# Layer 0 of a decoder: norms, transposes and rotary of the experts stage's first two groups in the cross attention's last turns

## The chip, the cores and the metric

The kernel runs on one core of one Trainium2 chip. Its time is the device time of one execution, in microseconds (us); the figure used is the median of several runs. The core's engines are called by their short names in the profile: PE (TensorE, matrix products and transposes), PEld (its weight loads), DVE (VectorE), ACT (ScalarE), POOL (GpSimd) and SP (SyncE, which here only issues transfers).

## The reference

A decoder of two layers works on x, an array of 32 sequences of 100 tokens with 256 features, all in float32. Each layer adds three sub-layers, each on a normed copy of x: a causal self attention, a cross attention, and a mixture of experts.

```python
x = x + attn(layernorm(x), ...)            # layer 0: causal, 16 heads of 16
x = x + xattn(ctx, layernorm(x), mask, ...)# 4 heads of 64, 361 context rows of 192
x = x + ffn(layernorm(x), ...)             # attention with rotary, then 8 experts
x = x + attn1(...); x = x + xattn1(...); x = x + ffn1(...)   # layer 1
```

Layer 0's cross attention norms the context and the latents (x) with gains, makes keys and values from both (361 + 100 rows), normalises each head of queries and keys by its root mean square, takes a masked softmax, and projects back. Layer 0's third sub-layer is a block of its own: rotary on the features, a causal attention of 16 heads whose queries and keys come from the rotated input and whose values come from the unrotated one, then a layer norm, a gate over 8 experts of which the two best count, and a last layer norm:

```python
q_in = apply_rope(x);  q, k, v = q_in @ Wq.T + bq, q_in @ Wk.T + bk, x @ Wv.T + bv
x1 = ln(x + softmax(causal(q @ k.T / 4)) @ v @ Wo.T + bo)
out = ln(x1 + sum_over_top2(gate * (x1 @ expert_w[e].T + expert_b[e])))
```

## The kernel before, in words

x stays in SBUF as eight tiles `xs[g]`, one for each group g of four sequences (100 token rows, four sequences, 256 features). The six sub-layers follow each other as stages: `a0` (self attention), `x0` (cross attention), `f0` (experts), then `a1`, `x1` and the experts of layer 1. The change touches `x0` and `f0` and a helper that `a0` and `f0` share.

**How order is set.** Inside a block `with in_order():` the instructions of PE, DVE, ACT and POOL go onto their engines in the order in which the program writes them, by hand. Across engines, and where a buffer is used again, the tile framework adds the waits. Outside of such blocks, and for SP, its scheduler places instructions. PSUM is cut into two `sc` tiles of two banks and four `mm` tiles of one bank, taken in turn. SBUF is given out by pools: a tile of a tag takes the next of that tag's buffers and waits until the last reader of what lay there is done. A pool opened where another was closed waits in the same way. Weight pools `w0`, `w1`, `w2` and so on are opened on alternating sides of SBUF; their loads are put on SP's queue when the pool is opened (`weight` and `plain`, transfers at L256 and L261).

**Stage x0.** `w2`, the pool with the experts stage's weights, is opened just ahead of `x0` and filled then, the 2 MB matrix of the experts (`f0_we`), the experts' biases (`f0_eb`) and the rotary table (`rope`) among them. The loop of `x0` has turns n from -4 to 32 (L851). In turn n, work of several sequences is interleaved, as a pipeline over b: keys of n+1 are transposed (`keys_turned`, PE L717 and L725, copies to kT by ACT L720 and to qT by DVE L728), the second half of n's softmax is divided (`divided`, DVE reciprocal L783 and POOL product L784), sequence n-1 is projected and added to x (`output`, PE L223, DVE L828, POOL L829), keys of n+2 are squared (ACT L681), and their roots taken (DVE L687, POOL L691), keys and values of n+3 made from latents (`own_keys_values`, ACT L671), n's weights transposed (`turn_weights`, PE L793, ACT L796), contexts of n+4 to n+6 normed and transposed, scores of n+1 made (`scores`, PE L751), n's weighted sums taken (`sums`, PE L807), and n+1's softmax begun (DVE L770, ACT L774). The turn ends with

```python
at(n + 1, exponentials, 1)
if out_:
    out_()
at(n + 1, divided, 0)
```

So `divided(n+1, 0)` is the last thing of turn n and `divided(n+1, 1)` an early one of the next turn, and their reciprocals are neighbours on DVE. From turn 26 on the pipeline has no new contexts to load, from turn 29 on no new keys to make.

**Stage f0.** `heads_attention` (L275) is the attention with 16 heads. Its prologue makes group 0's input by `norm(0, part)` for four parts, q and k of group 0 in four steps m (0 and 1 are q, 2 and 3 are k; PE L223, evacuations ACT L305 and L315), values and scores of sequence 0 and its softmax (DVE L365 and L376, POOL L377, ACT L382), and then all four parts of `norm(1, part)`. Its loop over turns s works on the weights of sequence s and the scores of s+1, and spreads q and k of the next group over turns: q in turns 0 and 1 of a group, both k in turn 2.

`norm(g, part)` in `f0` has these parts: part 0, statistics (four times DVE L161 and L162, DVE L170 and L173, POOL L174 and L176); part 1, the scaling of x to xl (four ACT L192); part 2, eight transposes (PE L945) with two copies to xlT (ACT L948); part 3, the rotary, four DVE instructions (L956, twice L958, L961), whose result xrT is what q and k are made from. The experts' matrix is first used in turn 9 of the stage, by `experts` (PE L1073).

Of the kernel before, what the change touches and what calls it, by code (L numbers as in the profile page):

```python
# [10 lines left out]
F32 = mybir.dt.float32  # L11
# [7 lines left out]
P = 128  # L19
# [47 lines left out]
def kernel(ctx: ExitStack, tc: tile.TileContext, io: dict, out: bass.AP):  # L67
# [207 lines left out]
    def heads_attention(pool, w, wo, bias, norm, turn, res, fill):  # L275
# [171 lines left out]
        with in_order():  # L447
            for part in range(4):
                norm(0, part)
# [9 lines left out]
            for part in range(4):  # L459
                norm(1, part)  # L460
            for s in range(B + 1 + fill.steps):
# [5 lines left out]
                if g < NG:  # L467
                    if i == 0:
                        turned_[g] = turn(g)
                    for m in ((0,), (1,), (2, 3), ())[i]:  # L470
                        queries_or_keys(g, m)
# [73 lines left out]
    f0_we = weight(w2, "f0_we", D, E * D)  # L545
    f0_eb = plain(w2, "f0_eb", [E, D])
    rope = plain(w2, "rope", [P, 3, T])
    kch = CCH + [(S2, T)]
    NK = S2 + T
    with tc.tile_pool(name="x0", bufs=2) as pool, tc.tile_pool(name="x0p", bufs=1) as fixed:  # L550
# [128 lines left out]
        def squares(b):  # L679
            sq = pool.tile([P, 5, D], F32, tag="sq", name="sq", bufs=1)  # L680
# [26 lines left out]
        def keys_turned(b, c):  # L707
            if c == 0:
                kTs[b] = [
                    pool.tile([P, 2, NK], F32, tag="kT", name="kT"),  # L710
                    pool.tile([P, 2, T], F32, tag="qT", name="qT"),
                ]
# [126 lines left out]
        with in_order():  # L839
# [11 lines left out]
            for n in range(-4, B + 1):  # L851
# [34 lines left out]
                at(n + 1, divided, 0)  # L886

# [37 lines left out]
    with tc.tile_pool(name="f0", bufs=2) as pool:  # L925
        xls = {}

        xrTs, xlTs = {}, {}

        def norm(g, part):  # L930


            if part == 0:
                xls[g] = stats(xs[g], G, tag="n", shift=True)
            elif part == 1:
                xl = pool.tile([T, G, D], F32, tag="xl", name="xl", bufs=3)
                scaled(xl, xs[g], G, xls[g])
                xls[g] = xl
            elif part == 2:
                xl2 = xls[g].rearrange("p g (d two) -> p g d two", two=2)  # L940
                xlT = xlTs[g] = pool.tile([P, 2, GT], F32, tag="xlT", name="xlT")
                for c in range(2):
                    ps = mm_tile()
                    for i in range(G):
                        nc.tensor.transpose(  # L945
                            ps[:, i * T : (i + 1) * T], xl2[:, i, :, c], ident[:T, :T]
                        )
                    nc.scalar.copy(xlT[:, c, :], ps[:, :GT])  # L948
            if part == 3:
# [1354 lines left out]
```

## Time and profile before

| what | us |
|---|---|
| median of 3 runs | 3555.65 |
| lowest and highest run | 3551.82, 3564.07 |
| the profiled execution | 3556.24 |
| its span (first to last instruction) | 3554.4 |
| busy: PE, DVE, ACT, POOL | 3353.6, 1873.7, 1602.8, 1258.7 |
| end of x0 (last residual add, L828) | 767.07 |
| first expert matmul of f0 (L1073) | 957.4 |

The mean granted clock of TensorE is 0.975. The profile is of one execution; its time differs from the span by 1.84 us, which lie around the instructions. In the timeline each line gives the start, the duration, the engine, the line of the kernel, the operation, what is written and read with shapes, and how many instructions the line stands for; in brackets follows how long the engine had been idle before it and what ended that. A line for several instructions gives the time that they were busy. A stretch of the windows view gives the same for each engine as sums.

### The profile page before, as it was taken

Reading aid. Unit: us, or ns where it says so; the run is one execution under the profiler, and the core shown is the slowest. Engines: PE = TensorE matmul, PEld = TensorE weight load, DVE = VectorE, ACT = ScalarE, POOL = GpSimd, SP = SyncE. Lnnn points to the kernel's source line nnn. Section 1 sums busy time; section 2 is a strip of 40 time slices with the busy share of each in tenths; the row PEclk is TensorE's granted clock in tenths of the full one; section 3 lists DMA queues with packets and bytes.
Section 4 is the critical chain, followed back from the end, with each engine's and each line's share of the span. In section 5 each row is a group of like instructions: output and inputs, shape, how many; then the busy total and the mean of one; then the engine's idle time right before and its main releaser. Section 6 shows DMA issues by size and latency. Waiting matters only on the chain. (4 is left out here: it accounts for less than half of the span.)

```text
span 3554.4 us, 66360 instructions
## 1 busy us (share of the span) xinstructions
PE 3353.6 (94%) x25978; PEld 2256.7 (63%) x25978; DVE 1873.7 (53%) x5328; ACT 1602.8 (45%) x3533; POOL 1258.7 (35%) x917
## 2 busy tenths in 40 slices
PE   7998999978989987999999999999999999999997
PEld 5775666646556643333466666666666668899997
DVE  6777777747676755755456464554646542011111
ACT  4664666646444414567454454545444442211111
POOL 3445887744444421000233333333233332012221
PEclk9999999989999998999999999999999999999999
DMA  2002000000101111000100000000000003466665
GB/s 84 2 2 64 23 26 23 16 17 9 28 22 31 27 38 47 1 1 1 41 14 19 19 25 21 20 26 19 20 27 18 25 13 111 140 178 184 187 179 146
DMA packets 109218, 168.15 MB, mean 47 GB/s; under 512 B 14996, under 2 KB 89628, under 8 KB 108444
## 3 DMA queue, kind: packets, MB, share of 16 engines
q1 hardware_dynamic: 94238, 145.60, 13.5%
q0 software_dynamic: 12688, 15.36, 2.4%
q8 instruction: 207, 3.39, 0.4%
q10 hardware_dynamic: 1982, 2.95, 0.2%
q14 instruction: 103, 0.84, 0.1%
HBM read 138.32 MB, written 28.82 MB: 47 GB/s over the span
## 5 line engine op out<-in xcount | busy, mean ns | idle before, releaser
L1696 POOL TENSOR_TENSOR ex<-ex,rc 100x1444 f32<-100x1444 f32 x128 | 332.1, 2594 | 785.1 <-DVE rc L1695 743.4
L1687 ACT ACTIVATE ex<-s,nmx 100x361 f32<-100x361 f32 x512 | 303.1, 594 | 143.4 <-DVE nmx L1678 143.4
L377 POOL TENSOR_TENSOR s<-s,nmx 100x800 f32<-100x800 f32 x128 | 210.1, 1641 | 332.4 <-DVE nmx L376 251.1
L1294 ACT ACTIVATE h<-sc,cols 128x800 f32<-128x800 f32 x256 | 222.4, 924 | 134.1 <-PE sc L1288 133.7
L1678 DVE CUSTOM_DVE_ANT_0 s<-sc,mb 100x361 f32<-100x361 f32 x512 | 250.5, 527 | 7.6 <-PE sc L1671 7.6
L2151 POOL DMA_INDIRECT acc_dram<-y,xg x57 | 89.0, 1562 | 451.1 <-DVE y L2150 243.0
L2133 ACT ACTIVATE hgT<-sc 128x1024 f32<-128x1024 f32 x57 | 58.4, 1024 | 351.2 <-PE sc L223 344.8
L1073 PE MATMUL mm<-xg,f_we 128*128 128x400 f32 x512 | 195.2, 527 | 19.3 <-ACT back L410 11.2
L223 PE MATMUL sc<-xgT,w1b 128*128 128x128 f32 x1824 | 213.1, 275 | 0.4 <-DMA w1b<-in_f_w 0.4
L2150 DVE TENSOR_SCALAR y<-mm,gx 128x256 f32<-128x256 f32 x57 | 27.6, 484 | 348.1 <-PE mm L223 348.1
L223 PEld LDWEIGHTS sc<-xgT,w1b 128*128 128x128 f32 x1824 | 208.2, 192 | 0.7 <-issue 0.6
L223 PE MATMUL mm<-wx,hgT 128*128 x912 | 206.1, 379 | 0.0
L1671 PE MATMUL sc<-kT,qT 64*100 64x361 f32 x1024 | 197.6, 463 | 0.0
L1643 PE MATMUL mm<-x_wa,cT 128*128 128x512 f32 (+1 forms) x512 | 191.1, 496 | 0.1
L1703 PE MATMUL mm<-ident,ex 100*128 100x100 f32 (+1 forms) x1536 | 168.0, 257 | 18.7 <-ACT kT L1625 9.7
L223 PEld LDWEIGHTS mm<-wx,hgT 128*128 128x128 f32 x912 | 169.0, 190 | 20.6
L1721 PEld LDWEIGHTS mm<-eT,vb 128*64 128x64 f32 (+1 forms) x3072 | 136.7, 137 | 67.4 <-issue 66.2
L1613 PE MATMUL mm<-cT,x_wa 128*128 128x361 f32 x512 | 178.1, 471 | 0.7 <-DVE lnT L148 0.7
L174 POOL TENSOR_TENSOR rs<-va,neghalf 100x4 f32<-100x4 f32 (+1 forms) x96 | 95.4, 997 | 216.9 <-DVE va L170 120.4
L1703 PEld LDWEIGHTS mm<-ident,ex 100*128 100x128 f32 (+1 forms) x1536 | 142.6, 151 | 39.8 <-ACT kT L1625 14.0
L1710 ACT COPY eT<-mm 128x400 f32<-128x400 f32 (+1 forms) x256 | 125.7, 491 | 89.2 <-PE mm L1703 87.7
L1721 PE MATMUL mm<-eT,vb 128*64 128x100 f32 (+1 forms) x3072 | 162.3, 254 | 0.0
(346 smaller groups left out, 7221.6 us busy)
## 6 DMA issues: line engine op xcount, KB each, us to landing
w1b<-in_f_w SPq DMA_DIRECT2D x57, 1024.0 KB
wb<-wt_dram SPq DMA_DIRECT2D x64, 200.0 KB
wx<-in_f_w SPq DMA_DIRECT2D x8, 1024.0 KB
xg<-sorted_dram SPq DMA_DIRECT2D x57, 132.5 KB
cb<-in_ctx SPq DMA_DIRECT2D x32, 192.0 KB
cT<-in_ctxT SPq DMA_DIRECT2D x32, 180.5 KB
cT<-in_ctxT SPq DMA_DIRECT2D x64, 90.2 KB
x<-in_x SPq DMA_DIRECT2D x8, 400.0 KB
```

Of the source, the lines that this page charges most:

```text
L223: nc.tensor.matmul(ps, lhsT[k], rhs[k], start=(k == 0), stop=(k == n - 1))
L377: nc.gpsimd.tensor_tensor(sm, sm, bc(nmx, 2, T), ALU.add)
L1073: nc.tensor.matmul(ps[:, :GT], f0_we[:, k, e * D + m * P : e * D + (m + 1) * P], xgs[E * g + e][:, k, :], start=(i > 0 and e == 2 * i and ...
L1294: nc.scalar.activation(h1, both[r2][:, :, :GT], AF.Tanh, bias=col("a1_b1", o))
L1613: nc.tensor.matmul(kTs[u][c][:, :S2], x1_wa[:, m * P : (m + 1) * P], cT[:, 0, :], start=True, stop=False,)
L1643: nc.tensor.matmul(ps[e][:kn, :n], cT[:, 0, at], x1_wa[:, 1024 + c0 : 1024 + c0 + n], start=True, stop=False,)
L1671: nc.tensor.matmul(ps[:T, e, :S2], qT[p0 : p0 + 64, m, tok], kT[p0 : p0 + 64, c, :], start=True, stop=True,)
L1678: nc.vector.tensor_tensor_reduce(s[:, e, :], ps[:T, e, :S2], mb, 1.0, 3.4e38, ALU.add, ALU.min, nmx[:, e : e + 1],)
L1687: nc.scalar.activation(ex[:, 2 * c + e, :], s[:, e, :], AF.Exp, bias=nmx[:, e : e + 1], scale=-1.0, accum_out=sm[:, 2 * c + e : 2 * c + e ...
L1696: nc.gpsimd.tensor_tensor(ex, ex, bc(rc, 2, S2), ALU.mult)
L1703: nc.tensor.transpose(pt[:kn, j * T : (j + 1) * T], ex[:, j, k0 : k0 + kn], ident[:T, :T])
L1721: nc.tensor.matmul(po[64 * e : 64 * e + 64, m * T : (m + 1) * T], vb[k][:kn, v0 + 64 * h : v0 + 64 * h + 64] if k < 2 else vb[2 + u % 2][: ...
```

## The change

Three things are changed. The matrix `f0_we` and the biases `f0_eb` are no longer loaded with the other weights of `w2` ahead of `x0`, but into a pool of their own when `f0` opens, where their transfers stand on SP's queue behind the weights of `a1`. The SBUF that this leaves free during `x0` is used by a pool `ahead`, open across `x0` and `f0`, for xl, xlT and xrT; for this kT and qT of `x0` have one buffer each instead of two, and the rotary's temporary in `x0` shares the buffer of the squares. And the function `norm` of `f0` is moved ahead, as `f0_norm`, and called at the end of turns of `x0` for groups 0 and 1: group 0's statistics in turn 24, its scaling in 25, group 1's statistics in 26 and scaling in 27, group 0's transposes in 29, its rotary and then group 1's transposes in 30, group 1's rotary in 31.

`heads_attention` takes `ready=2`: the prologue leaves both groups' norms out, and makes the two q steps of group 1 after the softmax of sequence 0; the k steps of group 1 follow in turns 0 and 1. Later groups are as before, and so is `a0`. No arithmetic is added or left out. In the diff the removed body of `norm` is left out, since it is that of `f0_norm`.

```diff
...
         load_x(g)
-    def heads_attention(pool, w, wo, bias, norm, turn, res, fill):
+    def heads_attention(pool, w, wo, bias, norm, turn, res, fill, ready=0):
...
             res(s, ps[:T, :D])
         with in_order():
-            for part in range(4):
+            for part in range(4 if ready < 1 else 0):
                 norm(0, part)
             turned_[0] = turn(0)
             for m in range(4):
...
                 masked(0, hf, ps[hf])
                 lowered(0, hf)
                 exponentials(0, hf)
-            for part in range(4):
+            if ready == 2:
+                turned_[1] = turn(1)
+                for m in range(2):
+                    queries_or_keys(1, m)
+            for part in range(4 if ready < 2 else 0):
                 norm(1, part)
             for s in range(B + 1 + fill.steps):
                 g, i = s // G + 1, s % G
...
                     ps = scores(s + 1)
                     masked(s + 1, 0, ps[0])
                 if g < NG:
-                    if i == 0:
-                        turned_[g] = turn(g)
-                    for m in ((0,), (1,), (2, 3), ())[i]:
-                        queries_or_keys(g, m)
+                    if g == 1 and ready == 2:
+                        for m in ((2,), (3,), (), ())[i]:
+                            queries_or_keys(g, m)
+                    else:
+                        if i == 0:
+                            turned_[g] = turn(g)
+                        for m in ((0,), (1,), (2, 3), ())[i]:
+                            queries_or_keys(g, m)
                 if i >= 1 and g + 1 < NG:
                     norm(g + 1, i - 1)
                 fill(s, 0)
...
     f0_w = weight(w2, "f0_w", D, 768)
     f0_wo = weight(w2, "f0_wo", D, D)
     f0_wg = weight(w2, "f0_wg", D, P)
-    f0_we = weight(w2, "f0_we", D, E * D)
-    f0_eb = plain(w2, "f0_eb", [E, D])
     rope = plain(w2, "rope", [P, 3, T])
+    ahead_cm = tc.tile_pool(name="f0e", bufs=2)
+    ahead = ahead_cm.__enter__()
+    xls, xrTs, xlTs = {}, {}, {}
+    def f0_norm(pool, tag, g, part):
+        if part == 0:
+            xls[g] = stats(xs[g], G, tag="n", shift=True)
+        elif part == 1:
+            xl = ahead.tile([T, G, D], F32, tag="xl", name="xl", bufs=3)
+            scaled(xl, xs[g], G, xls[g])
+            xls[g] = xl
+        elif part == 2:
+            xl2 = xls[g].rearrange("p g (d two) -> p g d two", two=2)
+            xlT = xlTs[g] = ahead.tile([P, 2, GT], F32, tag="xlT", name="xlT")
+            for c in range(2):
+                ps = mm_tile()
+                for i in range(G):
+                    nc.tensor.transpose(
+                        ps[:, i * T : (i + 1) * T], xl2[:, i, :, c], ident[:T, :T]
+                    )
+                nc.scalar.copy(xlT[:, c, :], ps[:, :GT])
+        else:
+            xlT = xlTs[g]
+            xrT = xrTs[g] = ahead.tile([P, 2, GT], F32, tag="xrT", name="xrT")
+            xwT = pool.tile([P, 5 * D], F32, tag=tag, name="xwT", bufs=1)
+            l4, r4, w4 = (
+                x.rearrange("p c (i t) -> p c i t", t=T)
+                for x in (xlT, xrT, xwT[:, : 2 * GT].rearrange("p (c t) -> p c t", c=2))
+            )
+            nc.vector.tensor_tensor(r4, l4, bc(bc(rope[:, 0], 1, G), 1, 2), ALU.mult)
+            for c in range(2):
+                nc.vector.tensor_tensor(
+                    w4[:, c], l4[:, 1 - c], bc(rope[:, 1 + c], 1, G), ALU.mult
+                )
+            nc.vector.tensor_tensor(r4, r4, w4, ALU.add)
     kch = CCH + [(S2, T)]
     NK = S2 + T
     with tc.tile_pool(name="x0", bufs=2) as pool, tc.tile_pool(name="x0p", bufs=1) as fixed:
...
             nc.vector.tensor_copy(vb[:T, 3, :], ps[:T, :D])
         def squares(b):
-            sq = pool.tile([P, 5, D], F32, tag="sq", name="sq", bufs=1)
+            sq = pool.tile([P, 5 * D], F32, tag="sq", name="sq", bufs=1)
+            sq = sq.rearrange("p (k d) -> p k d", d=D)
             nc.scalar.activation(sq, kbs[b], AF.Square)
             kns[b] = sq
...
         def keys_turned(b, c):
             if c == 0:
                 kTs[b] = [
-                    pool.tile([P, 2, NK], F32, tag="kT", name="kT"),
-                    pool.tile([P, 2, T], F32, tag="qT", name="qT"),
+                    pool.tile([P, 2, NK], F32, tag="kT", name="kT", bufs=1),
+                    pool.tile([P, 2, T], F32, tag="qT", name="qT", bufs=1),
                 ]
             kT, qT = kTs[b]
             kn_ = kns[b]
...
                 if out_:
                     out_()
                 at(n + 1, divided, 0)
+                for g_, part in {
+                    B - 8: ((0, 0),), B - 7: ((0, 1),), B - 6: ((1, 0),), B - 5: ((1, 1),),
+                    B - 3: ((0, 2),), B - 2: ((0, 3), (1, 2)), B - 1: ((1, 3),),
+                }.get(n, ()):
+                    f0_norm(pool, "sq", g_, part)
     def top2(pool, val, n, iota8, np_=T):
...
     a1_im = plain(w3, "a1_im", [P, P])
     a1_sum = plain(w3, "a1_sum", [P, 4, 32])
     a1_sel = plain(w3, "a1_sel", [P, 2, 32])
-    with tc.tile_pool(name="f0", bufs=2) as pool:
-        xls = {}
-        xrTs, xlTs = {}, {}
+    with tc.tile_pool(name="f0x", bufs=1) as fixed, tc.tile_pool(name="f0", bufs=2) as pool:
+        f0_we = weight(fixed, "f0_we", D, E * D)
+        f0_eb = plain(fixed, "f0_eb", [E, D])
         def norm(g, part):
...
+            f0_norm(pool, "xwT", g, part)
         def turn_group(g):
             return xrTs.pop(g), xlTs.pop(g)
...
             if n < E * NG:
                 tag = "xg" if n < 2 * (B - 2 * G) else ("xg", "xlT", "xrT")[(n // 2 + 1) % 3]
-                xg = pool.tile([P, 2, GT], F32, tag=tag, name="xg")
+                xg = (pool if tag == "xg" else ahead).tile([P, 2, GT], F32, tag=tag, name="xg")
                 nc.vector.tensor_tensor(xg, x1Ts[n // E], bc(wbs.pop(n), 1, 2), ALU.mult)
                 xgs[n] = xg
...
         fill.steps = 2 * G + 1
         heads_attention(
-            pool, f0_w, f0_wo, ("f0_bq", "f0_bk", "f0_bv"), norm, turn_group, res, fill
+            pool, f0_w, f0_wo, ("f0_bq", "f0_bk", "f0_bv"), norm, turn_group, res, fill, 2
         )
+    ahead_cm.__exit__(None, None, None)
     close_weights(2)
```

More of the change, by code (lines that the diff above doesn't have):

```diff
@@ L924 @@
     a1_sel = plain(w3, "a1_sel", [P, 2, 32])
-    with tc.tile_pool(name="f0", bufs=2) as pool:
-        xls = {}
-        xrTs, xlTs = {}, {}
+    with tc.tile_pool(name="f0x", bufs=1) as fixed, tc.tile_pool(name="f0", bufs=2) as pool:
+        f0_we = weight(fixed, "f0_we", D, E * D)
+        f0_eb = plain(fixed, "f0_eb", [E, D])
         def norm(g, part):
[L933 to L949, printed above, removed]
-                xlT = xlTs[g]
-                xrT = xrTs[g] = pool.tile([P, 2, GT], F32, tag="xrT", name="xrT")
-                xwT = pool.tile([P, 2, GT], F32, tag="xwT", name="xwT", bufs=1)
-                l4, r4, w4 = (
-                    x.rearrange("p c (i t) -> p c i t", t=T) for x in (xlT, xrT, xwT)
-                )
-                nc.vector.tensor_tensor(r4, l4, bc(bc(rope[:, 0], 1, G), 1, 2), ALU.mult)
-                for c in range(2):
-                    nc.vector.tensor_tensor(
-                        w4[:, c], l4[:, 1 - c], bc(rope[:, 1 + c], 1, G), ALU.mult
-                    )
-                nc.vector.tensor_tensor(xrT, xrT, xwT, ALU.add)
+            f0_norm(pool, "xwT", g, part)
         def turn_group(g):
```

## The prediction

> **What bounds the kernel now.** I read the share of each engine first (TensorE 94%), then the windows of the two stages that the change joins, and there the order of time. The columns of the windows: stretch and length, busy us (instructions) of PE, its weight loads, DVE, ACT, POOL, then granted clock, DMA share, GB/s.
>
> ```profile
> 400.00:700.00 300.00, 300.00 (x2341) 200.51 (x2341) 223.55 (x709) 190.03 (x449) 242.38 (x155) 1.00 0.09 22
> ...
> 735.00:767.00 32.00, 23.85 (x202) 16.04 (x198) 9.34 (x32) 16.11 (x43) 18.53 (x12) 0.86 0.00 1
> 767.00:784.00 17.00, 12.18 (x61) 6.89 (x60) 4.29 (x11) 6.77 (x12) 1.21 (x4) 0.65 0.27 83
> 784.00:805.00 21.00, 10.72 (x96) 7.47 (x96) 13.04 (x23) 8.39 (x15) 7.40 (x8) 0.59 0.00 0
> ```
>
> To turn 28 the cross attention is bound by TensorE without a gap (300.00 of 300; its residual add, L828, stands at 695.93, 710.01, 724.08: 14.07 us a turn). In its last turns nothing is left to fill TensorE with, and each waits for a chain. In the experts stage's first 38 us TensorE is half idle. So one microsecond put on a chain is lost in every part, unless it fits an idle time of that engine, and what is taken out at 767 to 805 is gained.
>
> The boundary, in order of time (start, us, engine, line, operation; in brackets the idle time before it and its releaser):
>
> ```profile
> 767.20 2.08 ACT L192 ACTIVATE xl<-x,sh,rs 100x256 f32<-100x256 f32 x4 [2.25 <-PE mm L223]
> ...
> 767.85 2.58 PE L945 MATMUL mm<-ident,xl 100*128 100x100 f32 x8 [0.82 <-ACT xl L192]
> ...
> 774.04 7.96 PE L223 MATMUL mm<-xrT,f_w 128*128 128x400 f32 x16 [3.60 <-DVE xrT L961]
> ...
> 782.79 0.96 PE L356 MATMUL sc<-kT,qT 32*100 32x100 f32 x32
> ...
> 792.13 2.58 PE L945 MATMUL mm<-ident,xl 100*128 100x100 f32 x8 [8.37 <-ACT xl L192]
> ...
> 798.31 3.03 PE L223 MATMUL mm<-xrT,f_w 128*128 128x400 f32 x4 [2.00 <-DVE xrT L961]
> ...
> 805.03 0.96 PE L356 MATMUL sc<-kT,qT 32*100 32x100 f32 x32
> ```
>
> Call E the end of the last cross attention output (767.04). Group 0's norm, transposes and rotary keep its first q matmul until E+7.0, scores(0) until E+15.75; then all of group 1's norm stands before turn 0, and scores(2) comes at E+38.0.
>
> **The change, part by part.** Sums are against the profiled execution, 3556.24 us (span 3554.4, 1.84 around it); the median of the runs is 0.59 less.
>
> *1. The start of the turns in the experts stage: the gain.* Both groups' q/k inputs are ready at E. The 16 q/k matmuls (7.96 us in the row; at the 0.39 us that they take from 778.8 on, not the 0.67 before, they would be 6.3) start at E, so scores(0) is at about E+8.2 instead of E+15.75. From scores(0) to the end of both exponentials the trace has 7.44 (782.79 to 790.23): E+15.65. Under them lie group 1's q matmuls (3.15) and scores(1). ACT then has four q evacuations (2.5), two exponentials (0.87 each) and four weight copies (1.67), which puts the copies at E+18.75 to 20.45 and scores(2) at about E+21.2: 16.8 us earlier. In turn 2 the k matmuls of group 1 are gone, since turns 0 and 1 took one each: 9.94 us (812.73 to 822.67) becomes some 8.4, ACT's scaling (2.06) then being its bound; 1.5 more. Together −18.5 (−15.5 to −19.5).
>
> *2. The head of the cross attention: a gain.* The 2 MB matrix stood ahead of the third and fourth context tiles on SP's queue, and DVE waited for one:
>
> ```profile
> 293.20 0.36 DVE L161 BATCH_NORM_STATS2 st<-cb 128x6 f32<-128x192 f32 x1 [2.51 <-DMA cb<-in_ctx]
> ```
>
> Followed through squares, roots and normed keys to the first key transposes at 310.38 (idle 3.04 before them), 1.7 of the 2.51 remain: −1.7 (0 to −2.5).
>
> *3. Stats, end of turns 24 and 26.* Ten DVE instructions (4 bn_stats, 4 bn_aggr, 2 small; 2.48 us in the row of group 1, 787.64 to 790.12) and two POOL ones (1.02, 0.20). They stand between the two reciprocals of the softmax division:
>
> ```profile
> 680.45 0.16 DVE L783 RECIPROCAL rc<-sm 100x2 f32<-100x2 f32 x1
> ...
> 680.78 3.41 POOL L784 TENSOR_TENSOR ex<-ex,rc 100x922 f32<-100x922 f32 x2 [2.90 <-PE mm L717]
> ...
> 680.95 0.17 DVE L783 RECIPROCAL rc<-sm 100x2 f32<-100x2 f32 x1 [0.34 <-ACT ex L774]
> ...
> 684.23 1.57 PE L793 MATMUL mm<-ident,ex 100*128 100x100 f32 x16
> ```
>
> The second reciprocal waits 0.34 now; with stats ahead it is at about 683.1. POOL does the pow and the product (1.22) from there, before the second division, which ends at about 686.3 instead of 684.19. TensorE's second pair of weight transposes moves from 684.43 to 686.35: +1.9, and as TensorE has no slack in these turns, it is kept, twice: +3.8 (2 to 5). Squares and roots on ACT and POOL shift inside the same wait. In the kernel before, group 0's stats lay in DVE's gaps at 685.94 to 689.0 at no cost; group 1's, at 787.64, are in part 1.
>
> *4. Scaling, end of turns 25 and 27.* Four ACT instructions (2.07) stand before squares (1.26) and key copies (0.97). ACT's idle times there, 0.68 and 0.57, hide 1.25; the rest delays the kb copy that the next transposes need: about 0.7 each, +1.4 (0.5 to 2.5).
>
> *5. Transposes, turns 29 to 31.* Group 0's eight (2.58) fall into TensorE's idle 2.60 before 746.29, with ACT copies (0.98) ahead of the key copies: +0.2. Group 1's lie under the chain of part 6.
>
> *6. Rotary, end of turns 30 and 31.* Four DVE instructions each (3.03 alone). The tail without them:
>
> ```profile
> 756.40 1.72 POOL L784 TENSOR_TENSOR ex<-ex,rc 100x922 f32<-100x922 f32 x1 [5.65 <-DVE rc L783]
> ...
> 758.24 0.17 DVE L783 RECIPROCAL rc<-sm 100x2 f32<-100x2 f32 x1 [2.01 <-ACT ex L774]
> ...
> 758.49 1.72 POOL L784 TENSOR_TENSOR ex<-ex,rc 100x922 f32<-100x922 f32 x1 [0.36 <-DVE rc L783]
> ...
> 760.26 1.45 PE L793 MATMUL mm<-ident,ex 100*128 100x100 f32 x14 [1.69 <-POOL ex L784]
> ```
>
> Group 0's rotary stands ahead of the reciprocal at 758.24, beside a POOL product. What such a meeting costs is in the stage itself:
>
> ```profile
> 827.00 4.00 POOL L377 TENSOR_TENSOR s<-s,nmx 100x800 f32<-100x800 f32 x1 [4.66 <-ACT eT L394]
> ...
> 827.67 0.98 DVE L956 TENSOR_TENSOR xrT<-xlT,rope 128x800 f32<-128x800 f32 x1
> ...
> 829.65 2.19 DVE L961 TENSOR_TENSOR xrT<-xrT,xwT 128x800 f32<-128x800 f32 x1
> ```
>
> POOL takes 4.00 instead of 1.52 (785.88), the last rotary add 2.19 instead of 0.99. So the rotary runs from 756.2 to about 760.9, the reciprocal comes at 761.0, and the last division starts at 761.15, is stretched by group 1's rotary from 761.4 on, and ends at about 764.9 instead of 760.21: +4.7 (2 to 5). The last weights, sums and output are behind it, so E moves by that.
>
> Here a rule differs from the row. The Trainium skill, "SBUF — State Buffer", section "Who interferes with whom", holds that a DVE instruction with two SBUF inputs and a GpSimd one that reads SBUF exclude each other, and that the one issued first keeps the ports for its whole length. By it the last division, started before the rotary, would end at 762.9: +2.6 in place of +4.7. In the row POOL started first (827.00) and was the one that was stretched, while DVE's 0.98 was at full speed. I take the row, and the rule's value as the low end.
>
> *7. At no cost.* The matrix's load, 2 MB behind the next stage's weights (SP done with them at 776.1): at the 242 GB/s of the head's DMAs some 9 us, landed near 790; its first matmul is at 957.4, so 165 us cover it, and the next transfer on SP's queue behind it is the gates' store at 878.91. One buffer each for kT and qT: TensorE, in its own order, issues the scores that read them (731.96) before the next key transposes (735.14), and the copies follow those. The x1 weights may load some 16 us earlier, before the next stage's end: off the path.
>
> Sum: E moves by −1.7 + 3.8 + 1.4 + 0.2 + 4.7 = +8.4; with −18.5 behind it −10.1: 3556.24 becomes 3546.1, the median 3555.65 about 3545.5.
>
> **The rivals.**
> - *Cheap insertions* (the exclusion as the rule has it, +2.6; stats at 1.2 a time): E moves by about +4, net −15, 3541. For it: DVE is 223.55 of 300 busy. Against: the order within each engine is fixed, and the places are on the chain.
> - *Dear insertions, small gain* (ends of 3, 4 and 6: +12.5; part 1 at −15.5; no gain at the head): −3, 3553. For it: ACT in the new start has q copies, exponentials and weight copies one behind another.
> - *Slower: the single kT/qT buffers bind.* If in the 32 turns the copies into kT wait for the last reader longer than the transposes already do, TensorE stops in each. The margin above is 1.4 us in turn 28. At 0.32 us a turn (32 x 0.32 = 10.2) the gain is gone, from 0.65 on (+20.8 −10.1) it is slower by more than the measurement; about 0.8 gives +15, 3571. Against it: the order of scores and transposes on TensorE.
> - *The change does not do what it says:* the matrix arrives late, or group 1's q matmuls gain nothing since ACT is behind. The first is excluded by 165 us; the second is in the third bullet's −15.5.
>
> **How the numbers follow.** A difference of 0.3% (10.7 us) is about what a measurement of this kernel can tell from none. The sum: 0.50, its own range −16 to −4 (3540 to 3552), of which 0.25 below −10.7; cheap insertions 0.22 (0.20 faster by more than that); dear ones 0.12, within it; slower 0.16 (0.15 past it). Faster 0.45, same 0.40, slower 0.15. The range 3534 to 3559 holds the first three but for their far ends; the slower case is left out.
>
> **What would show it.** L828 at turns 25 and 27 some 1.9 later, the second reciprocal of these turns 2 us behind the first; the last division ending 4 to 5 us later, with a POOL row near 3.7; E at about 775.4; no idle time at the first q matmul, scores(2) at about 21 behind E; turn spacing at 14.07 to turn 23. The prediction is wrong if that spacing grows, if the tail loses more than 8, or if scores(2) does not come within 24 of E.

## The result, and the profile after

The changed kernel takes 3542.69 us (median of 7 runs, 3539.95 to 3549.07), the kernel before in the same rounds 3555.96 (7 runs, 3551.82 to 3564.07): a ratio of 0.9959, 95% interval 0.9948 to 0.9969, or 13.3 us less. Forecast were 3545.5 and 10.1 us. The interval lies below 1, so the changed kernel is faster. The profiled execution of the changed kernel took 3541.43 (span 3539.7), 14.8 less than that of before.

Runs of one kernel differ. In the experiments the kernel before was run 70 times on four chips and fell into two groups, 3551.70 to 3559.28 with a mean granted clock of 0.975 to 0.977, and 3562.32 to 3569.23 with 0.972 to 0.974. Its median on a chip (3564.10, 3561.13, 3556.21, 3557.73) depends on how many runs fell into each. So the whole is read from ratios to the kernel before on the same chip, never from medians of different experiments, and single steps are read from stretches of the profiles.

The stretches below are differences of start times in each profile, in us. "Turns 25 to 28" is what these four turns take above those of before (14.08 us each, the fourth 13.15), counted from key transposes to key transposes. The changed kernel was profiled a second time, in an experiment further down; that column shows how much one kernel varies by itself.

| stretch | before | after | difference | forecast | after, second profile |
|---|---|---|---|---|---|
| end of self attention to first residual add of the cross attention | 58.91 | 55.39 | −3.52 | −1.7 | 55.96 |
| turns 25 to 28, excess | 0 | 4.54 | +4.54 | +5.2 | 4.53 |
| last key transposes to E, the last residual add | 20.78 | 23.30 | +2.52 | +4.9 | 23.57 |
| E to scores of sequence 2 | 37.96 | 18.64 | −19.32 | −16.8 | 20.62 |
| scores of sequence 2 to first instruction of the next stage | 537.12 | 539.02 | +1.90 | −1.5 | 533.78 |

With the 0.59 by which the self attention ended earlier, where nothing was changed, and 0.24 behind the experts stage, the differences make the span's 14.7. The last two rows differ between the two profiles of the changed kernel by 2.0 and 5.2 us, so the sign of the last one is not told.

The windows of the changed kernel, each shifted by the 3 us by which E is later (columns as in the prediction; the granted clock is third from the end):

```profile
400.00:660.00 260.00, 260.00 (x2030) 173.34 (x2028) 193.54 (x609) 163.71 (x387) 209.36 (x134) 1.00 0.09 23
738.00:770.00 32.00, 22.95 (x199) 17.57 (x200) 16.79 (x35) 15.59 (x40) 20.85 (x11) 0.84 0.00 1
770.00:787.00 17.00, 14.57 (x114) 8.89 (x113) 8.79 (x14) 8.79 (x15) 7.40 (x10) 1.00 0.60 205
787.00:808.00 21.00, 18.37 (x265) 13.66 (x265) 13.22 (x28) 13.72 (x27) 7.49 (x10) 0.92 0.01 3
```

The full turns are as before, the tail has 0.9 us less of TensorE in 32, and the two stretches at the start of the experts stage are filled: 14.57 of 17 and 18.37 of 21, where 12.18 and 10.72 stood. The granted clock in them went from 0.65 and 0.59 to 1.00 and 0.92 (0.94 and 0.83 in the second profile, over the same two stretches behind E). The start of the stage, from the timeline of the changed kernel (start, us, engine, line, operation; E is 770.10 here):

```profile
769.90 5.54 PE L223 MATMUL mm<-xrT,f_w 128*128 128x400 f32 x16
...
776.23 0.96 PE L357 MATMUL sc<-kT,qT 32*100 32x100 f32 x32
...
777.12 2.96 PE L223 MATMUL mm<-xrT,f_w 128*128 128x400 f32 x8
...
788.74 0.96 PE L357 MATMUL sc<-kT,qT 32*100 32x100 f32 x32
```

The q and k matmuls follow the last output without a wait and take 5.54 us, not the 7.96 of before, for the same 16. Scores of sequence 0 are at E+6.1 (forecast 8.2) and of sequence 2 at E+18.6 (forecast 21.2). From the same timeline turn 25, where group 0's statistics stand between the reciprocals:

```profile
676.40 0.16 DVE L831 RECIPROCAL rc<-sm 100x2 f32<-100x2 f32 x1
...
678.87 0.16 DVE L831 RECIPROCAL rc<-sm 100x2 f32<-100x2 f32 x1
...
680.21 1.72 POOL L832 TENSOR_TENSOR ex<-ex,rc 100x922 f32<-100x922 f32 x1
...
681.98 1.45 PE L841 MATMUL mm<-ident,ex 100*128 100x100 f32 x14 [0.47 <-POOL ex L832]
```

The reciprocals are 2.47 apart (0.50 before), the pow and product (678.97 to 680.25) stand before the second division, and the turn is 1.68 longer. And, again from the timeline, the last softmax beside the rotary:

```profile
755.74 3.27 POOL L832 TENSOR_TENSOR ex<-ex,rc 100x922 f32<-100x922 f32 x1 [3.81 <-DVE rc L831]
...
759.78 0.15 DVE L831 RECIPROCAL rc<-sm 100x2 f32<-100x2 f32 x1
...
760.01 3.69 POOL L832 TENSOR_TENSOR ex<-ex,rc 100x922 f32<-100x922 f32 x1 [1.00 <-DVE rc L831]
...
762.15 2.40 DVE L593 TENSOR_TENSOR xrT<-xrT,xwT 128x800 f32<-128x800 f32 x1
...
763.76 2.64 PE L841 MATMUL mm<-ident,ex 100*128 100x100 f32 x14 [4.30 <-POOL ex L832]
```

Both divisions, 1.72 before, take 3.27 and 3.69, and the last weight transposes start 3.50 later (760.26 before). Of these, 0.51 come from the turns ahead: the last key transposes are at 746.80, before at 746.29.

In the same tail TensorE's clock gave time back. Its last scores, sums and output are, in the timeline of the kernel before,

```profile
751.50 3.40 PE L751 MATMUL sc<-kT,qT 64*100 64x461 f32 x8
...
761.64 2.94 PE L807 MATMUL mm<-eT,vb 128*64 128x100 f32 x32
...
765.01 2.03 PE L223 MATMUL mm<-x_wo,oT 128*100 128x256 f32 x4 [0.42 <-ACT oT L817]
```

and in that of the changed kernel

```profile
752.01 1.80 PE L799 MATMUL sc<-kT,qT 64*100 64x461 f32 x8
...
766.32 2.21 PE L855 MATMUL mm<-eT,vb 128*64 128x100 f32 x32
...
768.96 1.11 PE L223 MATMUL mm<-x_wo,oT 128*100 128x256 f32 x4 [0.43 <-ACT oT L865]
```

The scores stand 5.21 us behind the last key transposes in both, but the granted clock from 751 to 755 us is 0.57 before and 1.00 after. So the first reciprocal of the last softmax comes 8.61 us behind these transposes (also in the second profile) and not 9.78. What raised the clock there was not tried by itself. The wait before the last key transposes is 2.60 before and 1.47 after, since group 0's transposes stand in it; in the four experiments below that take them out of that place it is about 2.6 again (2.59 to 2.61), and the scores take 3.30, 3.40, 2.64 and, in one, 1.79.

### The profile page after: what moved, and what is told of

It reads as the page before. It is cut to its first block, busy times and chain, and to the rows that moved or that the text cites. A ratio compares the mean times of both kernels' runs of the same rounds, so it can differ in the third digit from the quotient of the medians.

```text
span 3539.7 us, 66364 instructions
## 1 busy us (share of the span) xinstructions
PE 3347.8 (95%) x25978; PEld 2254.7 (64%) x25978; DVE 1876.3 (53%) x5328; ACT 1600.6 (45%) x3533; POOL 1261.8 (36%) x917
## 5 line engine op out<-in xcount | busy, mean ns | idle before, releaser
L1094 PE MATMUL mm<-xg,f_we 128*128 128x400 f32 x512 | 196.9, 530 | 19.3 <-ACT back L411 11.2
```

Of the source, the lines that this page charges most:

```text
L1094: nc.tensor.matmul(ps[:, :GT], f0_we[:, k, e * D + m * P : e * D + (m + 1) * P], xgs[E * g + e][:, k, :], start=(i > 0 and e == 2 * i and ...
```

## The experiments

**The load alone.** In the kernel before, the loads of `f0_we` and `f0_eb` move to a pool opened with the experts stage.

```diff
-    f0_we = weight(w2, "f0_we", D, E * D)
-    f0_eb = plain(w2, "f0_eb", [E, D])
...
+    with tc.tile_pool(name="f0x", bufs=1) as fixed, tc.tile_pool(name="f0", bufs=2) as pool:
+        f0_we = weight(fixed, "f0_we", D, E * D)
+        f0_eb = plain(fixed, "f0_eb", [E, D])
```

> The kernel before with the experts' matrix and biases alone moved to the opening of the experts stage. Theory (the context tiles come sooner, and TensorE's clock is not lowered by the wait): the first key transposes of the cross attention come 1.8 us earlier counted from the end of the self attention, the eight latent matmuls behind them take about 2.8 us and not 4.16, and the cross attention ends some 3.5 us earlier; nothing else moves, so about 3552.5 us. Rival (the 4.1 us seen at the head are the variation of the stage before): the cross attention's end moves by less than 1 us, 3556. Second rival (the matrix comes too late behind the other weights): the first expert matmul waits, and the experts stage is longer.

Measured: the first residual add comes 55.78 us behind the self attention (58.91 before), the cross attention's end 482.87 (486.13): −3.26. The first key transposes moved by −1.44 of these, most of the rest is in the lines that follow them. The timeline of the kernel before:

```profile
310.38 1.17 PE L717 MATMUL mm<-ident,kn 128*128 128x128 f32 x8 [2.84 <-POOL kn L701]
...
311.68 4.16 PE L223 MATMUL mm<-x_wl,lnT 128*100 128x512 f32 x8
```

That of the kernel with the load moved:

```profile
309.18 1.02 PE L715 MATMUL mm<-ident,kn 128*128 128x128 f32 x8 [2.04 <-POOL kn L699]
...
310.20 2.75 PE L223 MATMUL mm<-x_wl,lnT 128*100 128x512 f32 x8
```

The wait before them is 0.8 us shorter, and the eight latent matmuls run in 2.75 us, not in 4.16: the granted clock in the stretch from 300 to 317 is 1.00, and 0.90 in the kernel before. Of the 14 profiles taken, the eleven with the load moved have 2.75 us for the eight but once, the three without it 4.13 to 4.21. The first expert matmul is at E+124.3 (124.1 before): the matrix is not late. The ratio is 0.9996 (0.9984 to 1.0008), 3561.78 us; the profiled execution lost 7.3 us in the experts stage, where the code is the same, some 4 of them between 1134 and 1181 us, where the granted clock is 0.92 from 1090 to 1180 and 1.00 in the kernel before. So the gain is shown by the stretch, and the whole time can't tell it.

**One buffer each for kT and qT**, in the kernel before:

```diff
-                    pool.tile([P, 2, NK], F32, tag="kT", name="kT"),
-                    pool.tile([P, 2, T], F32, tag="qT", name="qT"),
+                    pool.tile([P, 2, NK], F32, tag="kT", name="kT", bufs=1),
+                    pool.tile([P, 2, T], F32, tag="qT", name="qT", bufs=1),
```

> The kernel before with one buffer each for kT and qT of the cross attention. Theory (the scores that read them stand ahead of the next transposes on TensorE): turns stay at 14.08 us, the end of the cross attention within 0.5 us, 3556. Rival (a wait in each turn): 0.3 us a turn and more, 3566 or above.

Measured: turns at 14.08 to the last, the cross attention's end at 485.40 (486.13), 0.7 earlier where at most 0.5 was expected, as the tail took 19.94 and not 20.78; 3558.54 us, ratio 0.9995 (0.9983 to 1.0007). The slower rival of the prediction rests on this wait, and there is none.

**The rotary back in the experts stage:**

```diff
-                    B - 3: ((0, 2),), B - 2: ((0, 3), (1, 2)), B - 1: ((1, 3),),
+                    B - 3: ((0, 2),), B - 2: ((1, 2),),
...
-            for part in range(4 if ready < 1 else 0):
+            for part in range(4) if ready < 1 else (3,):
                 norm(0, part)
...
             if ready == 2:
+                norm(1, 3)
                 turned_[1] = turn(1)
```

> The changed kernel with the rotary of both groups back in the experts stage: group 0's ahead of its q and k, group 1's behind the softmax of sequence 0. Theory (the rotary meets the POOL products of the last two turns): those products take 1.72 again and not 3.3 and 3.7, and the cross attention ends about 2.6 us earlier than in the changed kernel; the start of the experts stage pays 3.4 us for group 0 and 4 to 8 for group 1, so about 3548. Rival (the tail is later by the transposes and copies, not by the rotary): the end of the cross attention stays within 1 us of the changed kernel, 3550 or above.

Measured: both divisions at 1.72 again, the last key transposes to E 19.49 us (23.30): the rotary's place costs the tail 3.8, more than the whole tail's +2.5 of the changed kernel. The start pays for it: scores of sequence 0 at E+12.0, of sequence 2 at E+31.5, 12.9 later than in the changed kernel. 3550.02 us, ratio 0.9970 (0.9956 to 0.9984). By these stretches the early rotary is worth more than it costs even at its dear place; the ratios, whose intervals overlap, do not tell. The edit does not move quite all: the first multiplication of group 0's rotary still ran inside the cross attention, at 750.50, ahead of the last two divisions.

**Statistics and scaling in the idle times of a turn**, with the changed kernel's other parts kept:

```diff
+                for g_, part in {B - 6: ((0, 0),), B - 5: ((0, 1), (1, 0)), B - 4: ((1, 1),)}.get(n, ()):
+                    f0_norm(pool, "sq", g_, part)
                 at(n + 2, keys_normed)
...
-                    B - 8: ((0, 0),), B - 7: ((0, 1),), B - 6: ((1, 0),), B - 5: ((1, 1),),
```

> The changed kernel with statistics and scaling of both groups put where DVE and ACT are idle within a turn, ahead of the normed keys: group 0's statistics in turn 26 and scaling in 27, group 1's in 27 and 28. Theory (they cost only by standing between the two reciprocals, and ahead of the squares): turns 25 to 28 are back at 14.08, the cross attention ends 4.5 us earlier than in the changed kernel, about 3538. Rival (the engines have no free gap; POOL's two extra instructions delay the normed keys): turns 26 to 28 still grow by 1 us each, and 3541 or more.

Measured: all turns at 14.08, excess 0; the 4.54 us are the places, and none of it is the work. Nor is it the choice of turn: in turn 26 the statistics cost 1.68 at the end of the turn and nothing ahead of the normed keys, in turn 27 the scaling 0.59 and nothing. The tail, with the same instructions, took 24.24 (23.30 and 23.57), so the end came 3.45 earlier. Group 0's statistics in turn 26 of its timeline:

```profile
695.73 3.54 POOL L739 TENSOR_TENSOR rt<-ss,half 128x20 f32<-128x20 f32 x1
...
696.58 0.42 DVE L161 BATCH_NORM_STATS2 st<-x 100x6 f32<-100x256 f32 x1
...
698.90 0.17 DVE L173 TENSOR_SCALAR sh<-mv 100x4 f32<-100x4 f32 x1
...
699.31 0.18 DVE L746 TENSOR_SCALAR rn<-rt 128x20 f32<-128x20 f32 x1 [0.24 <-POOL rt L739]
```

They stand where DVE waits for POOL's roots, and DVE still waits 0.24 behind them. 3537.28 us (4 runs, 3536.87 to 3538.09), ratio 0.9930 (0.9909 to 0.9952).

**Group 1's rotary behind the last residual add:**

```diff
-                    B - 3: ((0, 2),), B - 2: ((0, 3), (1, 2)), B - 1: ((1, 3),),
+                    B - 3: ((0, 2),), B - 2: ((0, 3), (1, 2)), B: ((1, 3),),
```

> The changed kernel with group 1's rotary moved from the end of turn 31 to the end of turn 32, behind the last residual add; group 0's stays where it is. Theory (DVE's rotary and POOL's product of the softmax hold each other up): the last division takes 1.72 us and not 3.69, and the cross attention ends 2 us earlier than in the changed kernel; the product beside group 0's rotary keeps its 3.27. Group 1's q matmuls still find their input, so about 3540.7. Rival (the last division is late only since its reciprocal is): it still takes over 3 us, and the end moves by less than 0.5.

Measured: the division is as the theory has it, and the end as the rival has it (22.99 against 23.30). Its timeline, POOL's lines and then TensorE's:

```profile
757.15 3.27 POOL L832 TENSOR_TENSOR ex<-ex,rc 100x922 f32<-100x922 f32 x1 [4.49 <-DVE rc L831]
761.42 1.72 POOL L832 TENSOR_TENSOR ex<-ex,rc 100x922 f32<-100x922 f32 x1 [1.00 <-DVE rc L831]
...
763.20 2.64 PE L841 MATMUL mm<-ident,ex 100*128 100x100 f32 x14 [2.33 <-POOL ex L832]
765.76 2.94 PE L855 MATMUL mm<-eT,vb 128*64 128x100 f32 x32
769.12 2.03 PE L223 MATMUL mm<-x_wo,oT 128*100 128x256 f32 x4 [0.42 <-ACT oT L865]
```

Here the wait before the weight transposes fell from 4.30 to 2.33, the 1.97 that the theory gives. Behind them the sums take 2.94 and the output 2.03, where the changed kernel has 2.21 and 1.11: 1.65 went back to the granted clock, 0.68 from 757 to 772, where the changed kernel has 0.77. The 16 q and k matmuls took 6.42, not 5.54, and scores of sequence 0 came at E+7.03. 3545.23 us, ratio 0.9960 (0.9944 to 0.9976).

**Group 0's transposes and rotary in turn 29**, ahead of the weight transposes and of the normed keys:

```diff
+                for g_, part in {B - 3: ((0, 2),)}.get(n, ()):
+                    f0_norm(pool, "sq", g_, part)
                 for k in range(4):
                     at(n, turn_weights, k)
...
+                for g_, part in {B - 3: ((0, 3),)}.get(n, ()):
+                    f0_norm(pool, "sq", g_, part)
                 at(n + 2, keys_normed)
...
-                    B - 3: ((0, 2),), B - 2: ((0, 3), (1, 2)), B - 1: ((1, 3),),
+                    B - 2: ((1, 2),), B - 1: ((1, 3),),
```

> The changed kernel with group 0's transposes moved ahead of the weight transposes of turn 29, and its rotary into DVE's idle time of that turn, ahead of the normed keys; group 1's rotary stays at the end of turn 31. Theory: the first division of the last softmax takes 1.72 and not 3.27, the second reciprocal comes when the exponentials are done (2.7 us earlier), and the last division is stretched by group 1's rotary as before (3.7): the cross attention ends 2 to 2.8 us earlier than in the changed kernel, about 3540. Rival (DVE's gap in turn 29 is no gap, since POOL computes the roots in it): the normed keys come later, and the end moves by less than 1 us.

Measured: the last key transposes to E 20.95, 2.35 less, as expected, but by other terms. Both divisions were short, which saves 4.6 us between the first reciprocal and the last weight transposes; half of it was lost ahead of them, as the first reciprocal came 11.01 us behind the last key transposes (8.61 in the changed kernel), with the last scores at 2.64 us and not 1.80. POOL and DVE in the last turn of its timeline:

```profile
764.18 3.40 POOL L832 TENSOR_TENSOR ex<-ex,rc 100x922 f32<-100x922 f32 x2 [6.88 <-PE mm L576]
...
766.07 2.36 DVE L588 TENSOR_TENSOR xrT<-xlT,rope 128x800 f32<-128x800 f32 x1 [0.20 <-ACT xlT L579]
```

Both divisions keep 1.72, and now it is the rotary's first multiplication that takes 2.36 and not 0.98; before it DVE had waited for ACT's copy. The profiled execution also lost 3.3 us in the head (59.10, 55.78 with the load alone), where the latent matmuls took 4.93 behind a wait of 2.04, the same wait as in the others (granted clock 0.89 from 310 to 342; 1.00 at that place in the changed kernel), so its cross attention ended at 491.10, later than in the changed kernel (489.76): the part of the head's gain that is clock is not sure in each execution. 3544.37 us, ratio 0.9947 (0.9929 to 0.9965).

**Group 0 alone ahead:**

```diff
-            pool, f0_w, f0_wo, ("f0_bq", "f0_bk", "f0_bv"), norm, turn_group, res, fill, 2
+            pool, f0_w, f0_wo, ("f0_bq", "f0_bk", "f0_bv"), norm, turn_group, res, fill, 1
```

with group 1's parts taken out of the table of turns.

> The changed kernel with group 0 alone made ahead: group 1's four parts stand in the experts stage as before, ahead of turn 0. Theory (the start gains from each group by itself): scores of sequence 0 at 6.1 us behind the cross attention's end, but scores of sequence 2 at about 28.5 (38.0 less the 9.6 of group 0); the cross attention ends about 4 us earlier than in the changed kernel (half of the statistics, one rotary); about 3547 to 3548. Rival (group 1's norm hides under the softmax of sequence 0): scores of sequence 2 at 19 to 21, and the time at or below that of the changed kernel.

Measured: scores of sequence 0 at E+6.13, of sequence 2 at E+28.27; end of the cross attention 3.1 earlier than in the changed kernel; 3546.44 us, ratio 0.9961 (0.9948 to 0.9974). Each group brings about half: 9.7 of the 19.3 us for group 0 and 9.6 for group 1 (7.7 against the second profile of the changed kernel), whose norm does not hide under the softmax.

**Every part in an idle time:** the two edits of the statistics and of group 0's rotary together, group 1's transposes at the end of turn 30 and its rotary at the end of turn 32.

```diff
+                for g_, part in {B - 3: ((0, 2),)}.get(n, ()):
+                    f0_norm(pool, "sq", g_, part)
                 for k in range(4):
                     at(n, turn_weights, k)
...
+                for g_, part in {B - 6: ((0, 0),), B - 5: ((0, 1), (1, 0)), B - 4: ((1, 1),), B - 3: ((0, 3),)}.get(n, ()):
+                    f0_norm(pool, "sq", g_, part)
                 at(n + 2, keys_normed)
...
+                for g_, part in {B - 2: ((1, 2),), B: ((1, 3),)}.get(n, ()):
+                    f0_norm(pool, "sq", g_, part)
```

> The changed kernel with every part in an idle time: statistics and scaling of both groups in turns 26 to 28 ahead of the normed keys, group 0's transposes and rotary in turn 29 ahead of the weight transposes and the normed keys, group 1's transposes at the end of turn 30 and its rotary behind the last residual add. Theory: turns 25 to 28 at 14.08, both divisions of the last turn at 1.72, the cross attention's end 3.5 us earlier than in the kernel before by the head alone; the start of the experts stage as in the changed kernel; about 3534. Rival (the tail is bound by something else, or TensorE's clock falls in the longer waits): the end gains no more than the 3.5 us that the moved statistics gave, 3537 to 3538.

Measured: excess of the turns 0, last key transposes to E 20.65 (20.78 before), the cross attention's end at 483.05: the whole cost of the insertions, 6.7 us, is gone. Scores of sequence 0 come at E+7.09 and of sequence 2 at E+19.66, a microsecond later than in the changed kernel's first profile, since the 16 q and k matmuls took 6.54 and not 5.54; the experts stage took 558.5 (557.7). 3540.22 us (6 runs, 3538.31 to 3542.90), ratio 0.9942 (0.9927 to 0.9958). The stretch met the theory, the whole time only in part, and the lower clock of which the rival speaks has a share in that: with the insertions gone the wait before the last key transposes is back, and the last scores (3.30), the output (2.03) and the q and k matmuls ran at a lower clock again.

**The same with group 1's rotary at the end of turn 31**, and the changed kernel on the same chip:

```diff
-                for g_, part in {B - 2: ((1, 2),), B: ((1, 3),)}.get(n, ()):
+                for g_, part in {B - 2: ((1, 2),), B - 1: ((1, 3),)}.get(n, ()):
```

> As the kernel with every part in an idle time, but group 1's rotary at the end of turn 31, as in the changed kernel, so that the q and k matmuls are not behind a late residual add. Theory: the last division keeps 1.72 us, as where group 0's rotary alone was moved (there DVE was the one held up); the cross attention ends 3 us before that of the kernel before, scores of sequence 0 at 6.1 behind it; about 3536. Rival (the last division is stretched to 3.7 as in the changed kernel): its end 2 us later, 3538.

> The changed kernel as it is, beside its improvements on the same chip: 0.996 of the kernel before, and 4 to 7 us above the version with every part in an idle time. Its cross attention ends 489.8 us behind the self attention and its experts stage takes 557.7 up to the next stage, where the granted clock is the same.

Measured: the division kept 1.72 (the rotary's first multiplication took 2.11), the end at 482.96, but scores of sequence 0 at E+6.94 and not at 6.1, the q and k matmuls taking 6.40: 3539.85 us (5 runs, 3535.01 to 3545.19), ratio 0.9953 (0.9939 to 0.9967), against 3543.88 (6 runs, 3540.99 to 3546.48), 0.9968 (0.9956 to 0.9980), of the changed kernel beside it. The two intervals overlap: that the better places make the whole faster is shown by the stretch, and not by the time. The changed kernel's second profile has the end at 490.59, scores of sequence 2 at E+20.62 and an experts stage of 554.4: its first had 489.76, 18.64 and 557.7. So the last row of the table above (+1.90) is within what one kernel varies by: 533.8 from scores of sequence 2 on in this one, 539.0 in the first.

**TensorE kept busy at the start**, in the kernel before. Work is added that the result doesn't use:

```diff
+    def busy(n):
+        ps = mm_tile()
+        for _ in range(n):
+            nc.tensor.transpose(ps[:, :P], ident, ident)
...
+                if g == 0:
+                    busy(14)
...
+            if bias is not None:
+                busy(36)
             for part in range(4):
                 norm(1, part)
+                if bias is not None and part == 2:
+                    busy(10)
```

> The kernel before with added work: 14 transposes of the identity on TensorE behind group 0's transposes, 36 behind the first scores and 10 behind group 1's transposes, into a PSUM tile that nothing reads, so that TensorE is busy while it waits at the start of the experts stage. Theory (part of the start's cost is TensorE's lower granted clock behind its waits): q and k matmuls of group 0 take 6.3 us and not 7.96, the scores of sequence 2 come 2 to 3 us earlier than at 38.0, and the granted clock of the stretch is above 0.9. Rival (only the chain of norm, transposes and rotary counts): scores of sequence 2 at 38 or later by the added work.

Measured: the q and k matmuls of group 0 took 8.00, not 6.3, as the clock did not rise in time (0.62 from 767 to 784); from 784 to 805 it was 0.84 in place of 0.59, and scores of sequence 2 came at E+36.98, 1.0 earlier in spite of 60 added transposes (37.96 before; 38.20 and 38.50 in the two other profiles with the old start). 3555.51 us, ratio 0.9993 (0.9977 to 1.0009), no difference that can be told. So the clock has a share in the start's cost, about a microsecond of it within reach of this edit. How the rest divides this run does not tell: in the changed kernel, where the chain of norm and rotary is gone, the first 16 matmuls are also 2.4 us shorter by the clock.

**The rotary's input ready early**, to see which of DVE and POOL waits: as in the version with group 1's rotary at the end of turn 31, but with group 1's transposes before the weight transposes of turn 30.

```diff
-                for g_, part in {B - 3: ((0, 2),)}.get(n, ()):
+                for g_, part in {B - 3: ((0, 2),), B - 2: ((1, 2),)}.get(n, ()):
```

> As the version with every part in an idle time and group 1's rotary at the end of turn 31, but group 1's transposes and copies come before the weight transposes of turn 30, so that the rotary's input is there early and its first multiplication stands directly behind the residual add on DVE, some 0.2 to 0.4 us after the last division begins on POOL. Theory (a DVE instruction that is ready behind a running one takes its turn ahead of a POOL product that began less than a microsecond before; where it waited for ACT's copy, POOL kept its own): the last division takes 3.7 us, the multiplications 0.98 and 1.05, and the end of the cross attention is some 2 us later. Rival (whichever shows the earlier start keeps its turn): 1.72 us for the division, above 2 for the first multiplication.

Measured: neither the theory's number nor the rival's. The last division took 2.48 (752.44 to 756.60 for the two divisions), and DVE's lines of the timeline are

```profile
753.72 0.40 DVE L876 TENSOR_TENSOR x<-x,mm 100x256 f32<-100x256 f32 x1
754.03 0.98 DVE L588 TENSOR_TENSOR xrT<-xlT,rope 128x800 f32<-128x800 f32 x1
754.94 3.02 DVE L590 TENSOR_TENSOR xwT<-xlT,rope 128x400 f32<-128x400 f32 x2
```

The first multiplication began 0.09 before the division and was not held up; the division ended 1.59 behind it (755.01 to 756.60), and the next multiplication, 0.57 alone, waited for that end. The end of the cross attention is at 482.12, the earliest of all; 3538.09 us (4 runs, 3533.73 to 3542.72), ratio 0.9934 (0.9913 to 0.9956).

## Why the prediction was right

The direction and the size held: −10.1 forecast, −13.3 measured, within the likeliest case's own range (−16 to −4). The places that it named as costly are costly, and the start gains as it said.

Part of the number's fit is luck. The last residual add came at 770.10, 3.0 us later than before, and not at the forecast 775.4. What the sum lacks is, for the most part, TensorE's granted clock: it stands in the forecast only as an option for the first q and k matmuls, and gave some 1.4 us at the head, 1.6 in the tail and 2.4 at the start. And the rest of the experts stage, on which the forecast has −1.5, came out at +1.9 in one profile and at −3.3 in the other.

By its steps:

1. *The start.* Forecast −18.5 over the stage's opening, measured −19.3 up to scores of sequence 2 (−17.3 in the second profile), then no gain in turn 2: the two k matmuls fewer there did not shorten it (scores 3 to 4: 10.46, 9.94 before). The mechanism was right, two terms were mis-sized: the 16 q and k matmuls took 5.54 and not 7.96, as the clock was at full speed when the last output had run; and turn 2 gave nothing of its 1.5. That each group brings about half is shown by the run with group 0 alone.
2. *The head.* Forecast −1.7, measured −3.52, −3.13 with the load alone. The wait was sized rightly (−1.83 at the first key transposes, 310.38 less 307.96 and less the 0.59 of the stage before; the 3.04 of idle time that the step names is that of the weight loads, the matmuls waited 2.84). Missed were 1.4 us of clock in the latent matmuls behind it; the step has no term for it.
3. *Statistics.* Forecast +1.9 a time, measured +1.68 twice. 4. *Scaling.* Forecast +0.7 a time, measured +0.59 twice. That they cost by their place alone is shown: 0 in idle times.
5. and 6. *Transposes and rotary.* Forecast +4.9, measured +2.52. The row of the stage (4.00 for a product of 1.52) was the right measure for the meeting. Counted from the last key transposes, the meetings cost 4.2 us, near the forecast 4.7: the second reciprocal stands 4.37 behind the first (2.17 before), and the last division takes 3.69 (1.72 before). The clock gave 1.6 back, which the step had at nothing: 1.17 in the scores ahead of the first reciprocal, and 0.47 behind the last division, where the faster sums and output outweigh slower weight transposes (2.64, 1.45 before). By the Trainium skill ("SBUF — State Buffer", section "Who interferes with whom") the instruction that is issued first keeps the ports. Taken by the starts in the profile, that would have given 1.72 for the last division, which shows the earlier start (760.01 against 760.17), and it took 3.69; taking the row was right. That one of the two waits is as the rule says in each meeting; the recorded starts do not tell which.
7. *At no cost.* Shown for the single buffers (no wait in any turn) and for the matrix (first expert matmul E+124.3 with the load alone, E+124.1 before). That the x1 weights' earlier load does nothing was not tried by itself; the time from the experts stage's end on is 2211.96 (2212.20).

The rivals: by its number, the rival of cheap insertions did as well as the likeliest case or better. Its statistics at 1.2 and rotary at +2.6, put into the sum of the steps, give E +4.9 and −13.6 (the "about +4" and −15 of the prediction are not that sum), and the measured insertions come to +7.1, between its 6.6 and the likeliest case's 10.1. Its causes are not what was found: the statistics cost 1.68, and no division of the changed kernel's last softmax kept its 1.72. The insertions would be cheap at other places. The slower case fell with its wait.

## What to carry to other kernels

Work that is moved ahead into a full stage is free or dear by its place in each engine's order, not by its length: the same ten DVE, two POOL and four ACT instructions cost 2.27 us a group between two reciprocals and ahead of the squares, and nothing ahead of the normed keys, where these engines were idle. Sum the chain for each insertion, and look for the idle time of the very engine before fixing the place. What shortens a wait of TensorE may bring more than the wait, where the matmuls behind it run at a higher granted clock (the eight latent matmuls took 2.75 us behind a wait of 2.04, 4.16 behind 2.84). It is no rule: behind the same wait of 2.04 they once took 4.93.

## What was not expected of the hardware

The granted clock made several terms larger or smaller than the waits: eight latent matmuls in 2.75 or 4.16 us (4.93 once), an output of four in 1.11 or 2.03, and a wait shortened by 1.97 of which 0.31 was left. Two profiles of the same kernel differ as much: 539.0 and 533.8 us for the same rest of the experts stage, with scores of sequence 2 at E+18.64 and E+20.62.

Where DVE's rotary and POOL's products met in these runs, they did not both run at their full speed: one was held up by the other, and either could be the one. POOL's product waited for all three multiplications, although it shows a start 0.16, 0.67 or 0.74 us earlier than the first of them; it kept its 1.72 where that multiplication had waited for ACT's copy (starts 0.21 and 0.46 behind POOL's); and with the input ready early it waited for one multiplication and held up the next. What decides which goes first stays open; that an instruction queued ready behind a running one counts as earlier fits the first two and was not borne out by the number expected in the third.
